# Two layers of attention in one kernel: another order of the steps within a unit of the second layer

## The chip, the cores and the metric

The kernel runs on one core of one Trainium2 chip. The metric is the device time of one execution in microseconds (us). All arithmetic is in 32-bit floats. The engines have short names throughout, as in the profile: PE is TensorE (PEld its loads of weights), DVE is VectorE, ACT is ScalarE, POOL is GpSimd, SP is SyncE, which here only issues transfers.

## The reference

Eight images of 32 x 32 points with 512 channels pass through two layers.

```python
# layer 0: group norm, self-attention with 8 heads of 64 over the 1024 points, projection, residual
x = x + softmax(q k^T / 8) v @ w_out + b_out
# layer 1: deformable attention
x_ln = layernorm(x);  q = x_ln @ wq + bq
o = gelu(depthwise_conv_7x7_stride_2(q) + dw_b)        # 16 x 16 points
offsets = tanh(o @ pw)                                 # two numbers for each of the 256 points
interp = bilinear(x, refs + offsets)                   # 256 sampled points, 4 rows of x for each
k, v = (interp @ wv + bv) @ mk + .., @ mv + ..
z = softmax(qh kh^T) vh @ mo + mo_b + x                # 1024 queries, 256 keys, 8 heads
out = gelu(layernorm(z) @ mlp_w + mlp_b) + z
```

The second layer needs, for each image, the convolution of that image's queries, the offsets, the sampled rows, and from these the keys and values, before its first scores can be made.

## The kernel before, in words

The kernel makes the first layer for all images, writes its result (`mid`) and the normed result (`hat_d`) to memory, and then makes the second layer from these. The change touches the second layer alone (from line 838). The convolution of the first six images is made beside the first layer; that of the last two (`EARLY` is 6) is made in the second, beside the attention.

**Order.** Nothing is scheduled by a planner. Each engine runs its instructions in the order in which the program issues them (`InOrder`, lines 43 to 64; all operations are therefore recorded as line 54). The program makes this order by hand: `at(place, step)` (line 362) puts a step at a place, a number, and `run_due` (line 365) issues the steps by rising place. Equal places go by the order of entry. A step issues everything that it consists of at once, on whichever engines and queues. An engine that waits for something holds up everything behind it on that engine.

**Units.** The second layer has 64 units, numbered n. A unit is one pair of heads (`hp`, 4 of them) of one half image (`hi`, 16 halves of 512 queries). Its steps (`unit_steps`, line 1177) lie at places counted from n:

- n: `scores` (line 97). 32 matmuls into two tiles `sc`, one for each head; on DVE the negated maxima `nmax`, two reductions; on ACT the exponentials `e`, four for each head, with their sums.
- n + 0.02 and n + 0.04: `moved` (line 134) for head 0 and head 1. DVE transposes `e` into `sq` in blocks of 32; SP stores it to memory (`sq_d`) and loads it back, spread over partitions otherwise (`et`). `sq`, `e` and `et` have two buffers, one for each head.
- n + 0.039 and n + 0.041: `share` and `spread` (lines 164, 175): the reciprocal of the sums (`rs`, `rsT`) and its way through memory to `inv`.
- n + 0.06: `query_step` (line 1088): 16 matmuls that make the queries of unit n + 1, and ACT's `q` with its bias.
- n + 1.1 and n + 1.2: `product` (line 150), the matmuls `av` of exponentials and values, and `scale`, DVE's `attH`. These lie in the next unit.

**The end of a tile of rows** (`back_steps`, line 1096). Each unit also takes one tile t of 128 rows of the half image before through the end of the layer. Its places are counted from the tile's own n:

- n + 0.05: `joined` (line 1111): the output projection, 16 matmuls; DVE adds the residual (`z`), takes statistics and the variance (`stats`, `mv`), and POOL raises it to the power -0.5.
- n + 0.13: `norm`: DVE makes `zn`.
- n + 0.6: `turned` (line 1127): four transposes on PE, two copies `zT` on ACT.
- n + 1.03: `mlp`, 16 matmuls; n + 1.035: `biased`, DVE's `res`.
- for two tiles together, `gelu` at 1.72 and `end` at 2.24 after the second tile's n: ACT's gelu (with a table load before and after it), POOL's addition of `z` and the store of the result through POOL's queue.
- `fetch` and `add`, 1.6 and 0.5 ahead of a pair of tiles: SP loads two tiles of `mid` (`xr`) and POOL adds the bias row to them.

The results of matmuls take turns in three buffers `mm`.

**The convolution** (`conv_steps`, line 1204) runs in two lanes of taps, one tap for each of 49 weights. Lane 0 is on DVE, five taps at n + 0.25, or three in units where `points` holds. Lane 1 has seven taps in a unit: four at n + 0.045, three at n + 0.65 and on; each is a product on ACT (`parts`, two buffers) and an addition on POOL (`chunk`).

**The sampled points** (`point_steps`, line 1229). For image b let L = 8b - 4. At L - 0.035 comes the gelu of the convolution `o` on ACT; at L + 0.535 `offsets` (line 970): four pairs of matmuls, the tanh `th` on ACT and two small transposes on PE; at L + 0.75 `targets`, some 22 small operations on DVE (`corners`, line 1019) that make the rows' indices `ii` and weights `wt`. Then for each half h of the points `gather` (line 987), four indirect transfers through POOL's queue into `row` (four buffers), and `sample` (line 997), four DVE operations that add the weighted rows into `smp`: places L + 0.8 and L + 1.22 for the first half, L + 1.23 and L + 2.22 for the second. The keys and values of image b are made from `smp` from L + 3.18 on (`key_step`, `value_step`).

So for image 3, whose stretch is looked at below, L is unit 20.

Of the kernel before, what the change touches and what calls it, by code (L numbers as in the profile page):

```python
# [241 lines left out]
def attention_then_deformable_attention(  # L242
# [48 lines left out]
    def mm_tile():  # L291
        return ps_mm.tile([P, QB], F32, tag="mm", name="mm")
# [69 lines left out]
    def at(place, step):  # L362
        due.append((place, len(due), step))
# [474 lines left out]
    with ExitStack() as l1:  # L838
# [131 lines left out]
        def offsets(b):  # L970
            o = room[b, "o"]
            ps = mm_tile()
            for cb in range(NC):
                nc.tensor.matmul(
                    ps[0:2, 0:NS], lhsT=pww[:, cb, :], rhs=o[:, cb, :],
                    start=(cb == 0), stop=(cb == NC - 1),
                )
            th = cv.tile([2, NS], F32, tag="th", name="th")
            nc.scalar.activation(th, ps[0:2, 0:NS], AF.Tanh)
            room["th"] = mm_tile()[:, 0:4]  # L980
            for h in range(2):
                nc.tensor.transpose(room["th"][:, ts(h, 2)], th[:, ts(h, P)], ident[0:2, 0:2])

        def targets(b):
            room[b, "ii"], room[b, "wt"] = corners(room["th"])
# [24 lines left out]
        def points(b):  # L1010
            conv_load(b)
            conv_gelu(b)
            offsets(b)
            targets(b)
            for h in range(2):
                gather(b, h)
                sample(b, h)
# [78 lines left out]
        def back_steps(hi, start, step, tail=False):  # L1096

            b, half = divmod(hi, 2)
            xs = mid[b].rearrange("(t p e) c -> e t p c", e=2, p=P)[half]
            outs = out_tok[b].rearrange("(t p e) c -> e t p c", e=2, p=P)[half]  # L1100
            xr, z, zn, zT, res = {}, {}, {}, {}, {}
            n_units = 2 * B * NHP

            def fetch(t):
                xr[t] = tmp("xr", 4)
                nc.sync.dma_start(xr[t], xs[t])

            def add(t):
                nc.gpsimd.tensor_tensor(xr[t], xr[t], bo_row, ALU.add)

            def joined(t):
                ps = project(lambda c: attH[hi][:, c, ts(t, P)], lambda c: wo[:, c, :])
                z[t] = tmp("z", 4)
                nc.vector.tensor_tensor(z[t], ps, xr[t], ALU.add)
                stats = work.tile([P, 6], F32, tag="stats", name="stats")
                mv = xr["mv", t] = work.tile([P, 3], F32, tag="mv", name="mv")
                nc.vector.bn_stats(stats, z[t])
                nc.vector.bn_aggr(mv[:, 0:2], stats)
                rstd(mv[:, 2:3], mv[:, 1:2], 1e-5)

            def norm(t):
                zn[t], mv = tmp("zn", 2), xr["mv", t]
                nc.vector.tensor_scalar(
                    zn[t], z[t], mv[:, 0:1], mv[:, 2:3], ALU.subtract, ALU.mult
                )

            def turned(t):
                ps = mm_tile()
                for c in range(NC):
                    nc.tensor.transpose(ps[:, ts(c, P)], zn[t][:, ts(c, P)], ident)  # L1130
                zT[t] = tmp("zT", 2)
                for half in range(2):
                    nc.scalar.copy(zT[t][:, ts(half, C // 2)], ps[:, ts(half, C // 2)])

            def mlp(t):
                res["ps", t] = project(lambda c: zT[t][:, ts(c, P)], lambda c: wm[:, c, :])

            def biased(t):
                res[t] = tmp("res", 3)
                nc.vector.tensor_tensor(res[t], res["ps", t], bm_row, ALU.add)  # L1140

            def gelu(t):
                nc.scalar.activation(res[t], res[t], AF.Gelu)

            def end(t):
                (nc.vector if tail else nc.gpsimd).tensor_tensor(res[t], res[t], z[t], ALU.add)
                (nc.sync if tail else nc.gpsimd).dma_start(outs[t], res[t])

            for t in range(NC):
                over, eve = (start + step * t >= n_units - i and not tail for i in range(2))  # L1150
                n, pair = start + step * t, start + step * (t - t % 2)

                ends = (n + 0.6, n + 1.03, n + 1.035)
                if eve:
                    ends = (n + 0.61, n + 0.72, n + 0.73) if over else (n + 1.06, n + 1.62, n + 1.625)
                places = (pair - 1.6, pair - 0.5), (n + 0.05, n + 0.13), ends
                if tail:
                    turn = n + 0.15 + 0.005 * (t > 0)
                    places = (n - 0.7, n - 0.6), (n, n + 0.01), (turn, n + 0.25, n + 0.26)
                steps = (fetch, add), (joined, norm), (turned, mlp, biased)  # L1160
                for place, what in zip(sum(places, ()), sum(steps, ())):
                    at(place, lambda t=t, what=what: what(t))


                ends = [t - 1, t] if t % 2 and not tail else [t] if tail else []

                for what, after in (
                    (gelu, 0.27 if tail else 0.735 if over else 1.72),
                    (end, 0.28 if tail else 0.74 if over else 2.24),
                ):  # L1170
                    for i in ends:
                        at(n + after, lambda i=i, what=what: what(i))
# [4 lines left out]
        def unit_steps(n):  # L1177
            hi, hp = divmod(n, NHP)
            b = hi // 2
            u = dict(tiles=NQT, at=0, v=lambda j, h: vals[b][:, j, ds((2 * hp + h) * HD, HD)])  # L1180

            def scores():
                u["q"], u["k"] = queries.pop((hi, hp)), keys[b][:, hp, :]
                u["e"] = att.scores(u)

            def scale():
                if hp == 0:
                    attH[hi] = work.tile([P, NHP, QB], F32, tag="attH", name="attH")
                att.scale(attH[hi][:, hp, :], u["inv"])

            at(n, scores)
            at(n + 0.02, lambda: att.moved(u, 0))
            at(n + 0.039, lambda: att.share(u["sums"]))
            at(n + 0.04, lambda: att.moved(u, 1))
            at(n + 0.041, lambda: u.update(inv=att.spread()))
            last = n + 1 == 2 * B * NHP
            at(n + (1.3 if last else 1.1), lambda: att.product(u))
            at(n + (1.305 if last else 1.2), scale)
            if not last:
                at(n + 0.06, lambda: query_step(*divmod(n + 1, NHP)))  # L1200

        def conv_steps():
            for lane, chunks in enumerate(((0, 3, 6), (1, 2, 4, 5, 7))):
                free = 0.5 + lane
                for k in chunks:
                    b, cb = EARLY + k // NC, k % NC
                    first = next(n for n in range(60) if n + 0.49 > free)
                    fills = [first + 0.49, first + 0.55]  # L1210
                    at(fills[0] - 1.8, lambda b=b, cb=cb: conv_fetch(b, cb))
                    for par, place in enumerate(fills):
                        at(place, lambda b=b, cb=cb, par=par: fill(b, cb, par))
                        at(place + 0.02, lambda lane=lane, par=par: fill_end(lane, par))
                    unit = int(fills[1]) + 1
                    i = 0
                    while i < KS * KS:
                        points = unit % (2 * NHP) in range(NHP, NHP + 3)
                        count = 7 if lane else 3 if points else 5
                        for j in range(count):  # L1220
                            if i == KS * KS:
                                break
                            place = 0.25 + 0.01 * j if not lane else 0.045 + 0.001 * j if j < 4 else 0.65 + 0.01 * j
                            at(unit + place, lambda b=b, cb=cb, i=i, lane=lane: tap(b, cb, i, lane))
                            free = unit + place
                            i += 1
                        unit += 1

        def point_steps(b):
# [1 line left out]
            at(last - 1.5, lambda: conv_load(b))  # L1231
            at(last - 0.035, lambda: conv_gelu(b))
            at(last + 0.535, lambda: offsets(b))
            at(last + 0.75, lambda: targets(b))
            for h, (p0, p1) in enumerate(((0.8, 1.22), (1.23, 2.22))):
                at(last + p0, lambda h=h: gather(b, h))
                at(last + p1, lambda h=h: sample(b, h))
            first = 2 * NHP * b
# [79 lines left out]
```

## Time and profile before

| what | us |
|---|---|
| runs: median of 3 (lowest to highest) | 3460.95 (3454.47 to 3464.29) |
| the profiled execution | 3461.8 |
| its span (first to last instruction) | 3459.8 |
| PE busy 0 to 2000 | 1961.68 of 2000 |
| PE busy 2400 to 2600 | 194.36 of 200 |
| PE busy 2600 to 2800 | 181.57 of 200 |
| PE busy 2800 to 3000 | 181.88 of 200 |
| PE busy 3000 to 3400 | 392.69 of 400 |

The second layer's units run from 2233.07 (first scores) to the end. The lanes of taps end early in the stretch from 3000 to 3400.

How to read the profile: the page has one execution. A row of the timeline has the start in us from the beginning of the span, the duration in us, the engine, the line, the operation, the tiles (written <- read), the shape, and the number of instructions that are merged into the row. A bracket at the end gives the idle time before it and what ended that. A row of the waits has who waited for whom, the sum in us, how often, and the longest. The granted clock is the share of full speed that PE was given.

### The profile page before, as it was taken

To read this page: it belongs to the slowest core of one execution; us is meant where nothing else is said; L and a number is where in the kernel's file an instruction comes from. 1 tells how busy PE (TensorE), PEld (TensorE's weight loads), DVE (VectorE), ACT (ScalarE), POOL (GpSimd) and SP (SyncE) were. 2 spreads that over 40 slices of the span, in tenths; PEclk is the share of its full clock that TensorE was granted. 3 is DMA by queue.
4 is the path that set the end of the run, shared out by engine and by line. 5 is a ranking of instruction groups with operands and counts; after the bars stand their busy time and mean duration, and the time that the engine had idled before them with its cause. 6 is when DMAs were issued, how large, how long until landed. Compare 5 with 4: busy or idle time off the path is not lost.

```text
span 3459.8 us, 59748 instructions
## 1 busy us (share of the span) xinstructions
PE 3316.1 (96%) x21736; PEld 1352.4 (39%) x21736; DVE 2540.1 (73%) x3373; ACT 1809.4 (52%) x3919; POOL 1541.1 (45%) x1903
## 2 busy tenths in 40 slices
PE   7999999999999999999999998889998989899998
PEld 3444444444444444344344333333333333333332
DVE  4776787888888888888888884167777667565654
ACT  2443365575576576576576551245555555554442
POOL 1002226646646746746746754034535354532222
PEclk9999999999999999999999999899999999999999
DMA  4666767766766766766766775365656555565653
GB/s 145 174 178 166 208 174 201 210 176 189 216 176 182 226 175 179 229 181 179 217 181 179 214 201 167 126 195 183 209 167 190 164 185 190 177 205 187 218 181 125
DMA packets 446645, 642.57 MB, mean 186 GB/s; under 512 B 77104, under 2 KB 240944, under 8 KB 444304
## 3 DMA queue, kind: packets, MB, share of 16 engines
q1 hardware_dynamic: 415712, 536.67, 53.3%
q0 software_dynamic: 29488, 100.00, 9.5%
q8 instruction: 172, 2.82, 0.3%
q10 hardware_dynamic: 1152, 2.10, 0.2%
q14 instruction: 121, 0.99, 0.1%
HBM read 246.38 MB, written 123.73 MB: 107 GB/s over the span
## 4 chain that ended last, share of the span: by engine, by line
PE 78%; DVE 6%; ACT 5%; DMA 3%; POOL 3%; issue 2%; SPq 2%; DVEq 0%; POOLq 0%; ACTq 0%
PE mm L54 49%; PE sc L54 15%; PE av L54 14%; ACT e L54 3%; SPq L54 2%; POOL chunk L54 1%; DVE nmax L54 1%; DVE sq L54 1%; DMA et<-sq 1%; DVE chunk L54 1%; DMA sq_d<-sq 1%; POOL row L54 1%; DMA et<-sq_d 1%; ACT L54 1%; DMA row<-mid,ii 1%
## 5 line engine op out<-in xcount | busy, mean ns | idle before, releaser
L54 ACT ACTIVATE e<-sc,nmax 128x1024 f32<-128x1024 f32 (+1 forms) x1024 | 803.5, 798 | 574.3 <-DVE nmax L54 573.5
L54 DVE TENSOR_REDUCE nmax<-sc 128x1 f32<-128x1024 f32 (+1 forms) x640 | 751.5, 1215 | 308.5 <-PE sc L54 307.6
L54 DVE STREAM_TRANSPOSE sq<-e 128x1024 f32<-128x1024 f32 x640 | 764.2, 1225 | 246.7 <-ACT e L54 225.4
L54 POOL TENSOR_TENSOR oa<-part_x,oa 128x256 f32<-128x256 f32 x852 | 639.5, 751 | 549.7 <-ACT part_x L54 503.4
L54 ACT ACTIVATE part_x<-pad_x,dww_x 128x256 f32<-128x256 f32 x852 | 441.0, 544 | 251.9 <-POOL oa L54 250.6
L54 PE MATMUL sc<-k,q 64*64 64x512 f32 x4096 | 521.8, 602 | 20.5 <-ACT e L54 10.3
L54 PE MATMUL av<-et,v 128*64 128x256 f32 x4096 | 499.9, 386 | 12.7 <-DMA et<-sq 10.5
L54 PE MATMUL mm<-xT,wqkv 128*64 128x512 f32 x2048 | 463.8, 595 | 3.1 <-issue 3.1
L54 PEld LDWEIGHTS av<-et,v 128*64 128x64 f32 x4096 | 274.7, 137 | 329.1 <-issue 172.7
L54 POOL TENSOR_TENSOR chunk<-parts,chunk 128x256 f32<-128x256 f32 x240 | 180.8, 753 | 384.6 <-ACT parts L54 369.4
L54 POOL TENSOR_TENSOR mv<-mv,minus_half 128x1 f32<-128x1 f32 x128 | 76.0, 594 | 449.8 <-DVE mv L54 449.5
L54 PEld LDWEIGHTS sc<-k,q 64*64 64x64 f32 x4096 | 139.7, 132 | 329.3 <-issue 193.2
L54 PEld LDWEIGHTS mm<-xT,wqkv 128*64 128x64 f32 x2048 | 149.0, 138 | 255.0 <-issue 237.2
L54 PE MATMUL mm<-wm,zT 128*64 128x512 f32 x1024 | 236.0, 603 | 1.0 <-ACT zT L54 1.0
L54 DVE SCALAR_TENSOR_TENSOR od<-pad_x,dww_x,od 128x256 f32<-128x256 f32 x276 | 232.6, 843 | 5.5
L54 PE MATMUL mm<-wqkv,xT 128*64 128x256 f32 x2048 | 232.1, 379 | 0.0
L54 PE MATMUL mm<-wo,attH 128*64 128x512 f32 x1024 | 231.7, 593 | 0.4
L54 PE MATMUL mm<-hat_h,wqq 128*64 128x512 f32 x1024 | 231.5, 594 | 0.0
L54 PE MATMUL mm<-w,attT 128*64 128x512 f32 x1024 | 229.8, 592 | 1.6 <-DVE attT L54 1.6
L54 ACT ACTIVATION_READ_ACCUMULATOR e<-sc,nmax 128x1 f32 x1024 | 209.2, 204 | 0.0
L54 PEld LDWEIGHTS mm<-wqkv,xT 128*64 128x64 f32 x2048 | 147.7, 137 | 78.1 <-issue 6.4
L54 ACT ACTIVATE parts<-pad,dww 128x256 f32<-128x256 f32 x240 | 124.9, 557 | 91.2 <-POOL chunk L54 91.0
(163 smaller groups left out, 3446.8 us busy)
## 6 DMA issues: line engine op xcount, KB each, us to landing
et<-sq SPq DMA_DIRECT2D x2048, 128.0 KB
sq_d<-sq SPq DMA_DIRECT2D x128, 512.0 KB
et<-sq_d SPq DMA_DIRECT2D x128, 512.0 KB
inv<-rs_d SPq DMA_DIRECT2D x256, 128.0 KB
hat_h<-hat_d SPq DMA_DIRECT2D x16, 1024.0 KB
xr<-mid SPq DMA_DIRECT2D x64, 256.0 KB
x<-in_x_dram POOLq DMA_DIRECT2D x60, 256.0 KB
out_dram<-res POOLq DMA_DIRECT2D x60, 256.0 KB
```

Of the source, the lines that this page charges most:

```text
L54: return self.tc.keep_in_program_order(op(*args, **kwargs))
```

## The change

The order of the steps within a unit is changed, and the sampled points come later. From place to place:

- `joined` goes from n + 0.05 to n + 0.012 and `norm` from n + 0.13 to n + 0.03. On PE the projection now stands ahead of `mlp` (n + 0.03); on DVE `z`, its statistics and variance stand ahead of the first `sq`, and `zn` right behind it; POOL's power stands ahead of the four taps.
- `query_step` goes from n + 0.06 to n + 0.042: on ACT the bias of `q` stands ahead of the four taps at n + 0.045.
- `biased` goes from 0.035 to 0.0392: `res` stands behind the reciprocal, ahead of the second `sq`. It still follows its matmuls, which now come second.
- `offsets` is split. The two small transposes are a step of their own, `offsets_turned`, at L + 0.64, behind the turn of the normed tile, and ACT copies their result from PSUM to a tile in SBUF.
- `targets` goes from L + 0.75 to L + 1.041, behind the second `sq`. The gathers go to L + 1.05 and L + 2.05, which is behind the four taps of these units and ahead of the three at 0.65; the samplings go to L + 2.045 and L + 3.045, behind the second `sq` and ahead of `scale`.
- the units with three taps instead of five in lane 0 are one later.

```diff
@@ offsets
-            th = cv.tile([2, NS], F32, tag="th", name="th")
-            nc.scalar.activation(th, ps[0:2, 0:NS], AF.Tanh)
-            room["th"] = mm_tile()[:, 0:4]
+            room["tanh"] = cv.tile([2, NS], F32, tag="th", name="th")
+            nc.scalar.activation(room["tanh"], ps[0:2, 0:NS], AF.Tanh)
+
+        def offsets_turned(b):
+            th = room["tanh"]
+            ps = mm_tile()[:, 0:4]
             for h in range(2):
-                nc.tensor.transpose(room["th"][:, ts(h, 2)], th[:, ts(h, P)], ident[0:2, 0:2])
+                nc.tensor.transpose(ps[:, ts(h, 2)], th[:, ts(h, P)], ident[0:2, 0:2])
+            room["th"] = cv.tile([P, 4], F32, tag="th4", name="th4")
+            nc.scalar.copy(room["th"], ps)
@@ points
             offsets(b)
+            offsets_turned(b)
             targets(b)
@@ back_steps
-                ends = (n + 0.6, n + 1.03, n + 1.035)
+                ends = (n + 0.6, n + 1.03, n + 1.0392)
...
-                places = (pair - 1.6, pair - 0.5), (n + 0.05, n + 0.13), ends
+                places = (pair - 1.6, pair - 0.5), (n + 0.012, n + 0.03), ends
@@ unit_steps
-                at(n + 0.06, lambda: query_step(*divmod(n + 1, NHP)))
+                at(n + 0.042, lambda: query_step(*divmod(n + 1, NHP)))
@@ conv_steps
-                        points = unit % (2 * NHP) in range(NHP, NHP + 3)
+                        points = unit % (2 * NHP) in range(NHP + 1, NHP + 4)
@@ point_steps
-            at(last + 0.75, lambda: targets(b))
-            for h, (p0, p1) in enumerate(((0.8, 1.22), (1.23, 2.22))):
+            at(last + 0.64, lambda: offsets_turned(b))
+            at(last + 1.041, lambda: targets(b))
+            for h, (p0, p1) in enumerate(((1.05, 2.045), (2.05, 3.045))):
```

## The prediction

> **What bounds the kernel now.** I read the page's table of engines first, then TensorE's waits after 2100 us, then the timelines of four units.
>
> ```profile
> PE 3316.1 (96%) x21736; PEld 1352.4 (39%) x21736; DVE 2540.1 (73%) x3373; ACT 1809.4 (52%) x3919; POOL 1541.1 (45%) x1903
> ```
>
> TensorE is busy 96% of the span, so time is won only where it stands still or runs slowly. Its waits in the second pass (total us, times, longest):
>
> ```profile
> PE mm L54 <- DVE zn L54: 47.9, 15, 5.9
> PE av L54 <- DMA et<-sq_d: 13.4, 7, 4.7
> ...
> PE mm L54 <- ACT th L54: 3.7, 8, 0.5
> ...
> PE mm L54 <- DVE smp L54: 1.8, 1, 1.8
> ```
>
> Most of it is the turning of a normed tile (`zn`). TensorE's timeline shows where: units 21 and 22 of the loop (21 is the one after the offsets of image 3, L = 20).
>
> ```profile
> 2626.95 1.89 PE L54 MATMUL av<-et,vals 128*64 128x512 f32 x8
> 2633.64 0.72 PE L54 MATMUL mm<-ident,zn 128*128 128x128 f32 x4 [4.80 <-DVE zn L54]
> 2634.30 3.49 PE L54 MATMUL sc<-keys,q 64*64 64x256 f32 x32
> ...
> 2655.14 1.09 PE L54 MATMUL mm<-ident,zn 128*128 128x128 f32 x4 [5.19 <-DVE zn L54]
> 2656.16 3.69 PE L54 MATMUL sc<-keys,q 64*64 64x256 f32 x32
> ...
> 2672.61 3.80 PE L54 MATMUL mm<-smp,wvk 128*64 128x256 f32 x32
> ```
>
> The 32 score matmuls take 1.96 us in an unhindered unit (2595.90) and 3.49 and 3.69 here: the granted clock is 0.50 from 2655 to 2660. The last line, the keys, came without a wait. Behind all this stand ACT and POOL, which share the taps of the convolution:
>
> ```profile
> 2639.41 0.95 POOL L54 DMA_INDIRECT row<-mid,ii  x1 [0.30 <-DVE nmax L54]
> 2640.38 2.36 POOL L54 TENSOR_TENSOR chunk<-parts,chunk 128x256 f32<-128x256 f32 x3
> ```
>
> ```profile
> 2641.16 0.56 ACT L54 ACTIVATE parts<-pad,dww 128x256 f32<-128x256 f32 x1 [5.26 <-POOL chunk L54]
> 2641.73 1.28 ACT L54 ACT_TABLE_LOAD   x1
> 2643.03 1.15 ACT L54 ACTIVATE res<-res 128x512 f32<-128x512 f32 x2
> 2644.18 1.28 ACT L54 ACT_TABLE_LOAD   x1
> ```
>
> The third product of a group of three (`parts` has two buffers) waits for POOL's first add, that add stands behind the gathers in POOL's queue, and the exponentials stand behind the third product on ACT. So POOL's queue sets when the exponentials begin.
>
> **The change, part by part.** S is the start of a unit's scores. An unhindered unit has its product with the values at S+12.23 and its turn due at S+14.05 (2581.26, 2593.49, 2595.31), and lasts 14.64.
>
> Removed. *zn* comes after the first `sq` instead of after both. The projection now ends at S+5.3, `z`, its statistics and POOL's power take 2.5 (2590.35 to 2592.82), and `zn` is there soon after S+8.6, or after the exponentials of head 0 and one `sq`. Of the 15 waits, those with ordinary units behind them go. In unit L the tanh lies beside the turn (0.58), so the 7 waits of 0.46 go: 3.2. The slow matmuls after the waits: from turn to projection an undisturbed unit takes about 5.94 (2595.31, 2595.90, 2597.79, 2601.27); in the fifteen places the excess adds up to 20.0 (1.62 after 4.80; 2.94, 2.60, 2.60 and 2.87 after 5.19, 5.90, 5.59 and 3.96). All that could go: 47.9 + 3.2 + 20.0 = 71.1.
>
> Unit L+1. ACT now does the query's bias before the taps, so in unit L the four products start at S+13.2, POOL's adds end at 13.9 + 3.15 = 17.05; the two `res` adds, two stores and two `xr` adds take 6.8 (2612.11 to 2618.90); one add 0.8, third product 0.55: the exponentials of L+1 start at 25.2 of unit L, which lasts 16.7, so at S+8.5 (before: S+10.6, behind the indices on DVE). Head 0 takes 1.8, `sq` 1.25, `zn` 0.55: S+12.1, before the turn. **No wait.**
>
> Unit L+2. Both heads end at S+12.1 of L+1; reciprocal, its transpose, bias, second `sq`: 2.3; the index arithmetic, now behind them, 3.9 (2619.83 to 2623.78): S+18.3, which is S+3.7 of L+2. Four gathers, 5.2 (2624.06 to 2629.26), now stand *ahead* of the group of three adds: 8.9; add 0.8 and third product 0.55: 10.3; two table loads and two gelus, 3.75: exponentials at S+14.0, `zn` at 14.0 + 1.8 + 1.25 + 0.55 = 17.6. **3.6 us of wait remain** (5.2 to 5.9 before), three times, and some 2.0 once for image 2 with fewer adds: 12.8. L+3 starts at 18.2.
>
> Unit L+3. The exponentials of L+2 end at 17.6; bias and first product 1.2, four adds 3.15: 21.95; the second four gathers 5.2; `res`, stores, `xr` 6.8; one add and third product 1.35: 35.3, that is S+17.1 of L+3 (before S+9.0, since the gathers lay elsewhere). Exponentials 3.6, the 2.3 to the second `sq`: 23.0. Only then DVE samples the second half: four operations, 2.85 alone (2634.01 to 2636.85), and I add 0.6 for POOL's adds beside it (five taps 3.26 instead of 2.56): 26.4. The keys are due at S+14.05: **a new wait of 12.4 us**, in images 2 to 5: 49.6. Queued behind the keys on TensorE are the values, the turn and the next scores; nothing passes. Image 1 has no gelu and no stores: its exponentials start at S+10.3 in L+2, and 3.6 + 1.2 + 3.15 + 5.2 + 2.5 + 1.35 later, at S+12.7, in L+3; sampled at 22.05: a wait of 8. Images 6 and 7 have no taps on ACT; there `xr` lies behind gathers and stores until S+7.9, so `z` to second `sq` ends at 13.7, sampling at 16.5: 2.5 each, 5. Sum 62.6. Bounds of one wait of 12.4: 0 if the exponentials start right after the maxima (S+4.4); 15.7 with sampling at its slow 5.85 (2655.52 to 2661.37), gathers at 5.6, `res` to `xr` at 7.3.
>
> Slow matmuls after the new waits: 1.6 after each of four short ones, 2.75 (mean of the four rows above) after five long ones, 0.6 after two: 21.4.
>
> The Trainium skill, "TensorE: Matmul & The Clock Gate", section on what's actually happening, says that the clock halves after an idle window of about 3.4 us and returns after 3.4 busy ones. By that an estimate is 1.7 per wait over 3.4 and none below, so about 14 instead of 21.4, though 1.61 was lost at 2456.49 after a wait of 1.22. The skill's "SBUF — State Buffer", section on who interferes with whom, says that a VectorE operation with two inputs in SBUF is fully blocked by a GpSimd one that reads there; if four adds blocked sampling wholly, each long wait would be 2.5 longer, 10 in all. The taps' rows show a milder effect.
>
> Covered or small. The units with three instead of five taps on DVE move from L..L+2 to L+1..L+3: 1.0 us more ahead of the maxima of L+1, which then end near S+4.5, in the shadow of the exponentials' wait until S+8.5; without that cover it would cost up to 1.0 per image. The copy of the turned offsets is new on ACT; nearest rows are the tanh, 0.37, and a product, 0.53; it lies in POOL's wait: between 0 and +0.4 in each of 8 images, taken as 0. Moving four DVE operations ahead of `sq` delays the first half's store by up to 2.1 (S+6.5 to 8.6). SyncE's queue has the first `et` behind the store, and it waits for the product at S+14.2 anyway; the second store is queued behind that, so most units pay nothing. But in units 43 to 55 the first `et` comes at S+16 to 21, behind its store, and `av` waited 0.65 and 1.31 there. Ends: -3 (nothing added, those two gone) and +20 (2.1 in nine such units, and the last product, whose 4.5 of wait grow too). I take +5: 3 and 2.
>
> **Sum.** New 12.8 + 62.6 + 21.4 + 5.0 = 101.8; old 71.1; +30.7. The profiled execution took 3461.8 (span 3459.8): 3492.5. The median of the runs, 3460.95, is 0.9 lower, less than I can resolve.
>
> **Rivals.**
> *Faster: the exponentials aren't held.* For it: POOL is busy only 45%, and the keys had no wait before. Against it: the 5.26 above, at the same place in the queues. If the L+3 exponentials start by S+5, the keys find their data, and the 71.1 go, but for up to 19 that L+2 keeps (12.8 and four times 1.6): 3391 to 3410. If they start by S+9.5 the waits fall to about 4.8 and all is even; that is the point from which this rival decides.
> *About even*: the four long waits at 2.1 to 7.3 each, 3451 to 3472.
> *Worse*: slow sampling and gathers with store waits at their upper end: 4 x 3.3 + 15 more: 3521.
> That the order isn't what is said can be excluded: in the built program the gathers stand ahead of the adds and the sampling ahead of the scaling, in every image.
>
> **How the numbers follow.** Forecast case (3472 to 3510): 0.64; worse (to 3530): 0.11; even: 0.07; faster: 0.18. The likeliest time is 3492.5. The range from 3450 to 3522 leaves out the fast rival and the end of the worse one, with 0.2 between them. A measurement of this kernel can tell about 0.3% from no change, 10 us; faster 0.18, same 0.07, slower 0.75.
>
> **What would show it.** Right: TensorE's waits for `zn` fall from 47.9 to about 13 and the tanh line goes; "mm <- DVE smp" rises from 1.8 to 50 to 70 in eight or fewer waits; third products wait 15 us for POOL in L+2 to L+3; sampling ends near S+26. Wrong: keys that start at S+14 in L+3, or exponentials there before S+9.5; or waits for `et` in most units, which would show that the later `sq` does cost.

## The result and the profile after

The changed kernel takes 3483.12 us (median of six runs, 3477.66 to 3491.43), the kernel before 3462.18 (six runs beside them, 3454.47 to 3466.8): a ratio of 1.0064, interval 1.0048 to 1.008. It is slower, by about 21 us where 30.7 were forecast. The profiled execution took 3483.09, its span is 3481.4, against 3459.8 before: 21.6 more.

From the page of the changed kernel, the table of engines (busy us, share of the span, instructions):

```profile
PE 3319.0 (95%) x21736; PEld 1357.6 (39%) x21736; DVE 2473.5 (71%) x3373; ACT 1808.9 (52%) x3927; POOL 1542.9 (44%) x1903
```

TensorE's matmuls are the same number and busy 2.9 us longer. The other 18.7 are time in which it stands still, and its waits after 2100 us say for whom (total us, times, longest):

```profile
PE mm L54 <- DVE smp L54: 45.2, 7, 10.7
PE av L54 <- DMA et<-sq_d: 22.1, 9, 4.7
PE mm L54 <- DVE zn L54: 15.5, 4, 4.9
...
PE mm L54 <- ACT th L54: 0.9, 2, 0.5
```

The waits for `zn` fell from 47.9 to 15.5, and those for the tanh from 3.7 to 0.9. In their place stand the keys' waits for the sampled points: 45.2, of which 42.7 lie in the loop (10.62, 9.31, 10.71 and 10.13 in images 2 to 5, 1.14 and 0.81 in images 7 and 1) and the rest in the preparation. The waits for `et` rose by 8.7, and those of the scores for the queries `q` fell by 2.2 (3.5 to 1.3).

Image 3 shows how one unit after another is affected. L is unit 20, and its units have these lengths, from scores to scores:

| unit of image 3 | L | L+1 | L+2 | L+3 | sum |
|---|---|---|---|---|---|
| before | 18.47 | 19.93 | 21.86 | 24.20 | 84.46 |
| after | 16.67 | 14.64 | 19.52 | 36.50 | 87.33 |
| exponentials begin, before | S+8.2 | S+10.6 | S+11.2 | S+9.0 | |
| exponentials begin, after | S+9.0 | S+8.8 | S+14.7 | S+17.2 | |

L and L+1 gain 7.1 us, L+2 gains 2.3, and L+3 gives back 12.3. TensorE's timeline of L+2 and L+3 after the change (start, us, what; the bracket is the idle time before the row and what ended it):

```profile
2657.14 1.09 PE L54 MATMUL mm<-ident,zn 128*128 128x128 f32 x4 [4.38 <-DVE zn L54]
2658.15 3.69 PE L54 MATMUL sc<-keys,q 64*64 64x256 f32 x32
...
2672.48 2.44 PE L54 MATMUL av<-et,vals 128*64 128x512 f32 x7
...
2675.18 0.61 PE L54 MATMUL mm<-smp,wvk 128*64 128x256 f32 x2
2685.11 5.59 PE L54 MATMUL mm<-smp,wvk 128*64 128x256 f32 x28 [9.31 <-DVE smp L54]
```

The keys of image 3, which had found their data before the change, stand still for 9.31 us and then run slowly (5.59 us for 28 matmuls, where the 32 of before took 3.80; the granted clock is 0.52 from 2685 to 2690). What held the points is read backwards. First POOL's timeline of the same stretch:

```profile
2658.26 3.54 POOL L54 TENSOR_TENSOR chunk<-parts,chunk 128x256 f32<-128x256 f32 x4 [7.13 <-ACT parts L54]
2661.95 1.27 POOL L54 DMA_INDIRECT row<-mid,ii  x1 [0.15 <-issue]
...
2671.67 2.50 POOL L54 TENSOR_TENSOR xr<-xr,bo_row 128x512 f32<-128x512 f32 x2
2674.12 2.35 POOL L54 TENSOR_TENSOR chunk<-parts,chunk 128x256 f32<-128x256 f32 x3
```

Between the four adds and the three stand the gathers (2661.95 to 2667.27), then `res`, two stores and `xr` (to 2674.12): 12.2 us of other work in POOL's queue. ScalarE waits for just that:

```profile
2674.89 0.53 ACT L54 ACTIVATE parts<-pad,dww 128x256 f32<-128x256 f32 x1 [12.48 <-POOL chunk L54]
2675.32 0.45 ACT L54 ACTIVATE e<-sc,nmax 128x256 f32<-128x256 f32 x1
```

The third product waits 12.48 us for POOL's first add to free a `parts` buffer, and the exponentials begin right behind it, at S+17.2. VectorE makes the two `sq` from them, and only then samples the second half:

```profile
2681.18 0.82 DVE L54 TENSOR_SCALAR smp<-row,wt 128x512 f32<-128x512 f32 x1
2682.04 3.01 DVE L54 SCALAR_TENSOR_TENSOR smp<-row,wt,smp 128x512 f32<-128x512 f32 x3
```

It ends at 2685.05, S+26.9, and the keys start. So the gathers, now ahead of the group of three adds, hold the exponentials, and the sampling, now behind the second `sq`, takes over their lateness. The same gathers hold the sampling by a second path too, which is only 2.5 us shorter: `xr` stands behind them in POOL's queue, `z` waits 5.55 us for it on VectorE (to 2672.98), and `z` with its statistics (to 2674.80) stands ahead of both `sq`. The exponentials let the first `sq` start at 2677.27.

### The profile page after: what moved, and what is told of

The parts are those of the page before. It is cut to its first block, busy times and chain, and to the rows that moved or that the text cites. A ratio compares the mean times of both kernels' runs of the same rounds, so it can differ in the third digit from the quotient of the medians.

```text
span 3481.4 us, 59722 instructions
## 1 busy us (share of the span) xinstructions
PE 3319.0 (95%) x21736; PEld 1357.6 (39%) x21736; DVE 2473.5 (71%) x3373; ACT 1808.9 (52%) x3927; POOL 1542.9 (44%) x1903
## 4 chain that ended last, share of the span: by engine, by line
PE 74%; ACT 7%; DVE 5%; POOL 4%; DMA 4%; issue 3%; SPq 2%; another core or an unknown queue 0%; DVEq 0%; POOLq 0%; ACTq 0%
PE mm L54 47%; PE sc L54 14%; PE av L54 13%; ACT e L54 4%; SPq L54 2%; DVE sq L54 2%; DMA et<-sq 1%; DVE nmax L54 1%; DMA sq_d<-sq 1%; POOL chunk L54 1%; DVE smp L54 1%; DMA et<-sq_d 1%; POOL xr L54 1%; ACT L54 1%; POOL res L54 1%
## 5 line engine op out<-in xcount | busy, mean ns | idle before, releaser
L54 PE MATMUL av<-et,v 128*64 128x256 f32 x4096 | 499.8, 386 | 17.4 <-DMA et<-sq 13.3
```

What stands on the lines that cost most here:

```text
L54: return self.tc.keep_in_program_order(op(*args, **kwargs))
```

## The experiments

All edits are given against the changed kernel. The ratios are to the kernel before, run beside each.

| kernel | median us (range) | ratio (interval) |
|---|---|---|
| changed | 3483.12 (3477.66 to 3491.43) | 1.0064 (1.0048 to 1.008) |
| order_alone | 3431.81 (3427.86 to 3433.31) | 0.9913 (0.989 to 0.9936) |
| points_alone | 3520.05 (3512.41 to 3522.55) | 1.0169 (1.0141 to 1.0196) |
| gather_behind_taps | 3454.89 (3448.39 to 3461.2) | 0.9987 (0.9975 to 1.0) |
| sample_first | 3430.5 (3424.85 to 3433.29) | 0.991 (0.9885 to 0.9934) |
| offsets_alone | 3468.22 (3458.98 to 3475.62) | 1.0014 (1.0 to 1.0028) |
| fewer_taps | 3440.11 (3435.7 to 3442.99) | 0.9936 (0.9917 to 0.9955) |
| order_fewer_taps | 3420.87 (3419.53 to 3428.04) | 0.9888 (0.9869 to 0.9907) |
| sample_fewer_taps | 3424.84 (3418.7 to 3429.7) | 0.9897 (0.9879 to 0.9915) |
| norm_alone | 3437.33 (3427.0 to 3439.64) | 0.9915 (0.9888 to 0.9942) |
| sample_between | 3420.38 (3420.1 to 3420.6) | 0.9874 (0.9853 to 0.9895) |

The theory is the one of the prediction: the queues of POOL and VectorE carry the loss, the new order of projection and norm is a gain. The main rival was that the later transposes of exponentials (and with them the store and `et`) cost the time.

**order_alone**: the new order of projection, norm, query and bias stays, the points go back to their places.

```diff
-                        points = unit % (2 * NHP) in range(NHP + 1, NHP + 4)
+                        points = unit % (2 * NHP) in range(NHP, NHP + 3)
...
-            at(last + 1.041, lambda: targets(b))
-            for h, (p0, p1) in enumerate(((1.05, 2.045), (2.05, 3.045))):
+            at(last + 0.75, lambda: targets(b))
+            for h, (p0, p1) in enumerate(((0.8, 1.22), (1.23, 2.22))):
```

> The changed kernel with the index arithmetic, gathers, samplings and the three-tap units at their old places (0.75; 0.8 and 1.22, 1.23 and 2.22); the order of projection, norm, queries and bias, and the split offsets, stay. The queue theory (the loss is the keys waiting for samples that stand behind exponentials that stand behind gathers in POOL's queue): keys don't wait, zn waits fall from 47.9 to 15 to 25 in units L+1 and L+2, 3425 to 3445. The rival that the later transposes of exponentials cost (their stores and loads come later): waits of the products for et rise and the time is 3462 or more.

It is faster than the kernel before by 0.9%, within the range expected. Its two largest waits of TensorE in the second layer:

```profile
PE av L54 <- DMA et<-sq_d: 22.3, 13, 4.6
PE mm L54 <- DVE rs L54: 10.7, 3, 3.6
```

The second line is the wait of the turn, put down to the instruction behind `zn` on VectorE: three waits, and one of 2.3 for `zn`, where the kernel before has fifteen of 47.9 together. Five waits of 6.6 us together for `res` are new. The waits for `et` are as long as in the changed kernel. So the later transposes cost some 9 us of waiting (22.3 against 13.4) and the slow matmuls behind it, and still this half of the change is a gain of 29 us: as the cause of the loss, the rival falls.

**points_alone**: the other half, with projection, norm, query and bias back at their places.

```diff
-                ends = (n + 0.6, n + 1.03, n + 1.0392)
+                ends = (n + 0.6, n + 1.03, n + 1.035)
...
-                places = (pair - 1.6, pair - 0.5), (n + 0.012, n + 0.03), ends
+                places = (pair - 1.6, pair - 0.5), (n + 0.05, n + 0.13), ends
...
-                at(n + 0.042, lambda: query_step(*divmod(n + 1, NHP)))
+                at(n + 0.06, lambda: query_step(*divmod(n + 1, NHP)))
```

> The changed kernel with projection, norm, queries and bias at their old places; the later points and the split offsets stay. The queue theory: the exponentials of L+2 and L+3 are as late as in the changed kernel, and zn, now again behind both transposes, waits for them too, so it is slower than the changed kernel: 3495 to 3525, with zn waits of 70 to 100. The rival that the order does the harm: 3455 to 3470.

It is 1.7% slower than before. The points' new places cost 59 us by themselves, and here the cost shows as waits for `zn`:

```profile
PE mm L54 <- DVE zn L54: 98.7, 18, 10.3
```

The keys wait for nothing in its loop: in image 3 TensorE has stood still 10.32 and 5.76 us at the turns before them. Against the same runs of before (3460.63) order_alone is 29 us below and points_alone 59 above, 30 together, where the whole is 21 above. The split of `offsets` is in both halves and so counted twice (by offsets_alone, below, it is 0 to 10 us slower by itself), so whether the halves also hide each other's time can't be told.

**gather_behind_taps**: the gathers go behind the three adds of their units.

```diff
-            for h, (p0, p1) in enumerate(((1.05, 2.045), (2.05, 3.045))):
+            for h, (p0, p1) in enumerate(((1.715, 2.045), (2.715, 3.045))):
```

> The changed kernel with both gathers issued behind the group of three taps of their unit (places 1.715 and 2.715 instead of 1.05 and 2.05), the samplings unmoved. The queue theory: exponentials of L+2 start some 5 us earlier (near S+8) and of L+3 too, zn waits go to 0 to 5, the keys' waits fall from about 10 to 6 to 9, 3445 to 3462. The rival that only the sampling's place behind the second transpose matters and POOL's queue does not: 3475 to 3490, keys' waits as before.

It is 28 us below the changed kernel: the whole loss goes, and the waits for `zn` with it. The time is as expected, but the keys' waits hardly fall:

```profile
PE mm L54 <- DVE smp L54: 44.4, 6, 10.5
```

In the loop they are 5.71, 8.99, 8.93, 10.48 and 8.06 in images 1 to 5: 9.1 in the mean of images 2 to 5, where the changed kernel has 10.2 and 6 to 9 were expected, and image 1 has 5.71 instead of 0.81. In image 3 the exponentials of L+3 start at S+12.7 instead of S+17.2, and the second half is sampled at S+24.3 instead of S+26.9; but L+3 itself begins without the wait and the slow matmuls of L+2, so its keys are due sooner. POOL's queue shows where the gathers stand now:

```profile
2659.43 2.41 POOL L54 TENSOR_TENSOR chunk<-parts,chunk 128x256 f32<-128x256 f32 x3
2662.00 1.02 POOL L54 DMA_INDIRECT row<-mid,ii  x1 [0.15 <-issue]
...
2666.81 0.58 POOL L54 TENSOR_TENSOR mv<-mv,minus_half 128x1 f32<-128x1 f32 x1
```

Of the 12 us that lay ahead of the three adds the gathers were 5; `res`, the stores and `xr` (2652.11 to 2659.43) stay there. And the gathers now hold something else: POOL's power `mv` stands behind them and ends at 2667.39, `zn` starts at 2667.43, and the second `sq` and the sampling follow `zn` on VectorE.

**sample_first**: the samplings go ahead of what they stood behind, and the second gathers follow the first sampling.

```diff
-            for h, (p0, p1) in enumerate(((1.05, 2.045), (2.05, 3.045))):
+            for h, (p0, p1) in enumerate(((1.05, 2.015), (2.016, 2.3))):
```

> The changed kernel with the first half sampled ahead of both transposes of L+2 (2.015), the second half gathered at once behind it (2.016) and sampled at 2.3, in the same unit's end. Queue theory and the rival of the sampling's place: the keys find their samples, no wait at the keys, zn waits of 12 to 25 stay (the first gather still stands ahead of the three taps), 3425 to 3445. The rival of the later transposes: 3470 or more.

As expected. The keys have no wait for their samples in the loop, L+3 of image 3 lasts 23.41 instead of 36.50, and a wait of 5.63 for the turn stands in L+2 (23.0 in all images, 12 to 25 expected): 53 us less than the changed kernel, by the places of two steps on VectorE's and POOL's queues.

**offsets_alone**: of the whole change only the split of `offsets` is kept; these are the edits of order_alone and points_alone together.

```diff
-                ends = (n + 0.6, n + 1.03, n + 1.0392)
+                ends = (n + 0.6, n + 1.03, n + 1.035)
...
-                places = (pair - 1.6, pair - 0.5), (n + 0.012, n + 0.03), ends
+                places = (pair - 1.6, pair - 0.5), (n + 0.05, n + 0.13), ends
...
-                at(n + 0.042, lambda: query_step(*divmod(n + 1, NHP)))
+                at(n + 0.06, lambda: query_step(*divmod(n + 1, NHP)))
...
-                        points = unit % (2 * NHP) in range(NHP + 1, NHP + 4)
+                        points = unit % (2 * NHP) in range(NHP, NHP + 3)
...
-            at(last + 1.041, lambda: targets(b))
-            for h, (p0, p1) in enumerate(((1.05, 2.045), (2.05, 3.045))):
+            at(last + 0.75, lambda: targets(b))
+            for h, (p0, p1) in enumerate(((0.8, 1.22), (1.23, 2.22))):
```

> The kernel before with the split offsets alone (transposes behind the turn of the normed tile, the copy to SBUF on ACT). Every theory: the seven waits of 0.46 for the tanh go in the loop and nothing else changes, 3455 to 3463. If the copy in the preparation costs, the first scores start later than 2233.07 by up to 1.5.

A miss: no gain, 1.0014 (1.0 to 1.0028), and a median 5 us above the expected range. Six of the seven waits of 0.46 for the tanh are gone (image 1 keeps its own, as no tile is turned in its unit L), but the waits for `zn` rise from 47.9 to 54.0. TensorE's timeline in unit L of image 3 has this:

```profile
2616.11 0.63 PE L54 MATMUL mm<-ident,zn 128*128 128x128 f32 x4 [1.94 <-DVE zn L54]
```

The turn starts 1.94 us after the products of the offsets end (2614.17). In the kernel before it was 1.96 (2611.84 to 2613.80), with the 0.46 for the tanh inside. `zn` sets the turn in both, so what a wait ahead of it gives is lost at the next. The 3.2 us that the prediction put down as removable by the split were not there to be won, as long as `zn` is late. The first scores start at 2235.86, 2.8 later than before; but in the other kernels with this same preparation they start anywhere between 2233.35 and 2241.13, so a price of the copy in the preparation can't be read from it.

**fewer_taps**: lane 1 has five taps instead of seven in units L+1 and L+2, so that POOL's second group there is one add; the other taps come in later units.

```diff
-                        count = 7 if lane else 3 if points else 5
+                        two = unit % (2 * NHP) in range(NHP + 1, NHP + 3)
+                        count = (5 if two else 7) if lane else 3 if points else 5
```

> The changed kernel with five taps in lane 1 instead of seven in units L+1 and L+2: the second group has one tap, not three, so no product in it waits for an addition behind the gathers. The taps left out come in later units; the sum of work is the same, and the gathers and samplings stay where the change put them. The queue theory: the exponentials of L+2 start near S+9 instead of S+14.7 and those of L+3 at S+8 to 12 instead of S+17.2, zn waits go to 0 to 3, the four long keys' waits fall to 4 to 8, 3440 to 3460. The rival that the sampling's place and not the products' wait holds the exponentials: exponentials as late as before, 3478 to 3486.

With one product in the second group none waits for POOL behind the gathers. The exponentials of image 3 start at S+8.5, S+7.5 and S+6.7 in L+1 to L+3 (S+8.8, 14.7 and 17.2 in the changed kernel), and the time falls by 43 us. That is the strongest evidence for the queue: every gather and sampling is where it was and the work is the same; only two products a unit, one of which waited for the queue, are elsewhere. The waits of TensorE after 2100 us:

```profile
PE av L54 <- DMA et<-sq_d: 36.4, 14, 5.3
PE mm L54 <- DVE smp L54: 14.1, 6, 6.2
```

In the loop the keys' waits are down to 7.9 from 42.7 (one of 6.2 lies in the preparation), and the turn has none. But the exponentials of L+3 come 10.5 us earlier and the sampling ends only 4.5 us earlier, at S+22.4. VectorE's timeline of L+3 in image 3 shows the second path from POOL's queue:

```profile
2656.12 0.69 DVE L54 TENSOR_TENSOR z<-mm,xr 128x512 f32<-128x512 f32 x1 [6.28 <-POOL xr L54]
```

`z` waits for `xr`, which stands behind the gathers, until S+14.1, and both `sq` and the sampling stand behind `z`. The waits for `et` rise to 36.4 from 22.1. In L+3 of image 3 TensorE waits 3.47 us for it, where it was not late at all. It belongs to the second `sq` of L+2, whose store stands behind these two in SyncE's queue:

```profile
2638.98 0.32 SPq L54 DMA_DIRECT2D sq_d<-sq  x1
2645.31 0.37 SPq L54 DMA_DIRECT2D et<-sq_d  x1
```

The load is issued 6.3 us after the store on which it waits; in the changed kernel it was 2.65 (2656.59 to 2659.24). In images 2 to 5 it is 6.3 to 8.0 against 2.65 to 3.4. With earlier exponentials the store follows the loads of `xr` by 1.5 to 3.7 us, where it followed by 7.8 to 10.4; whether it shares their time, or that of the gathers, was not tried.

**order_fewer_taps**: order_alone, and five taps in units L and L+1, where its gathers are.

```diff
-                        points = unit % (2 * NHP) in range(NHP + 1, NHP + 4)
-                        count = 7 if lane else 3 if points else 5
+                        points = unit % (2 * NHP) in range(NHP, NHP + 3)
+                        two = unit % (2 * NHP) in range(NHP + 0, NHP + 2)
+                        count = (5 if two else 7) if lane else 3 if points else 5
...
-            at(last + 1.041, lambda: targets(b))
-            for h, (p0, p1) in enumerate(((1.05, 2.045), (2.05, 3.045))):
+            at(last + 0.75, lambda: targets(b))
+            for h, (p0, p1) in enumerate(((0.8, 1.22), (1.23, 2.22))):
```

> The new order with the old places of the points (as in order_alone), and five taps instead of seven in lane 1 in units L and L+1. The queue theory: what order_alone had left, exponentials at S+12 to 14 in L+1 to L+3 and their waits for rs and zn (about 3.6 each), goes for the most part, 3412 to 3425. If these waits come from the index arithmetic on DVE alone, it stays at 3428 to 3434.

The time is as expected, and 1.1% faster than the kernel before. The waits did not go for the most part: those of the turn are 7.4 in three (2.4 to 2.5 each), down from 10.7 (3.6 each) and the one of 2.3; image 3 takes 74.99 us (16.67, 17.11, 17.41, 23.80) against 84.46.

**sample_fewer_taps**: sample_first with the taps of fewer_taps.

```diff
-                        count = 7 if lane else 3 if points else 5
+                        two = unit % (2 * NHP) in range(NHP + 1, NHP + 3)
+                        count = (5 if two else 7) if lane else 3 if points else 5
...
-            for h, (p0, p1) in enumerate(((1.05, 2.045), (2.05, 3.045))):
+            for h, (p0, p1) in enumerate(((1.05, 2.015), (2.016, 2.3))):
```

> The changed kernel with the samplings ahead (as in sample_first) and five taps instead of seven in lane 1 in units L+1 and L+2. The queue theory: exponentials of L+2 and L+3 start at S+8 to 11 instead of S+11 to 15, the waits at the turn of 4.4 to 6.1 go, 3410 to 3425. The rival as above: 3426 to 3434.

The time lies at the upper end of what was expected, and the mechanism expected was wrong: the exponentials of L+2 are early (S+7.5), but the turn of that unit still waits 5.42. VectorE's timeline of L+2 in image 3:

```profile
2634.82 0.75 DVE L54 SCALAR_TENSOR_TENSOR smp<-row,wt,smp 128x512 f32<-128x512 f32 x1 [0.67 <-DMA row<-mid,ii]
2635.49 1.24 DVE L54 STREAM_TRANSPOSE sq<-e 128x1024 f32<-128x1024 f32 x1
```

Each operation of the sampling but the first waits for its rows, the last until 2634.82, and `sq` and `zn` (2636.65) stand behind it, with their data long there. The wait was the rows', not the exponentials'.

**norm_alone**: order_alone, with the query's bias and `res` also back at their old places; only `joined` and `norm` stay moved, and the split.

```diff
-                ends = (n + 0.6, n + 1.03, n + 1.0392)
+                ends = (n + 0.6, n + 1.03, n + 1.035)
...
-                at(n + 0.042, lambda: query_step(*divmod(n + 1, NHP)))
+                at(n + 0.06, lambda: query_step(*divmod(n + 1, NHP)))
```

(and the places of the points as in order_alone)

> As order_alone, but with the queries and the bias at their old places too: only projection and norm go ahead of the transposes (and the offsets are split). If these two carry the order's gain, it is as fast as order_alone, 3427 to 3438. If the queries' place has a share in it, slower, 3440 or more.

As expected: 0.9915, where order_alone has 0.9913. The projection and the norm carry the whole gain, as far as these runs can tell. The scores have ten waits for the queries, 17.0 in all, where order_alone has two of 1.3 together, but `et` waits 15.8 instead of 22.3; a difference between the two can't be told.

**sample_between**: the sampling of the first half behind `zn` and ahead of the reciprocal, the second gather right after it, and the taps of fewer_taps.

```diff
-                        count = 7 if lane else 3 if points else 5
+                        two = unit % (2 * NHP) in range(NHP + 1, NHP + 3)
+                        count = (5 if two else 7) if lane else 3 if points else 5
...
-            for h, (p0, p1) in enumerate(((1.05, 2.045), (2.05, 3.045))):
+            for h, (p0, p1) in enumerate(((1.05, 2.035), (2.036, 2.3))):
```

> As sample_fewer_taps, with the first sampling behind zn and ahead of the second transpose (2.035, second gather 2.036) instead of ahead of zn (2.015). The queue theory: the turn's waits of about 5.5 in L+2 (16 to 21 in all, put down to rs) go, since zn no longer stands behind the sampling; the keys stay without long waits: 3400 to 3415. If those waits came from late exponentials instead, it stays at 3419 to 3430.

It is the fastest of all with 3420.38, level with order_fewer_taps, and some 5 us above the expected range. The time alone would fit the rival (3419 to 3430), but the turn's waits, which the rival would have kept, are gone, and L, L+1 and L+2 of image 3 take 16.67, 14.64 and 14.64. What stayed is in L+3 (28.34), on VectorE:

```profile
2643.52 1.49 DVE L54 TENSOR_SCALAR smp<-row,wt 128x512 f32<-128x512 f32 x1
2645.04 6.56 DVE L54 SCALAR_TENSOR_TENSOR smp<-row,wt,smp 128x512 f32<-128x512 f32 x3
```

The second half's sampling takes 8.05 us here, alone 2.85, and the maxima of L+3 (2651.53) stand behind it, so the exponentials start at S+16.9. And the first half's sampling, which waits for rows, now stands ahead of `res`: TensorE has seven waits of 13.3 us together for `res` to empty a buffer `mm`, which the changed kernel has not. Four of them, 8.4 us, come early in L+3, behind that sampling: there the wait for the rows has moved from `zn` to `res`. The other three, 1.6 each, lie among the keys, behind the late exponentials.

## Why the prediction was right, and where its sizes were off

**Side and mechanism** were right. The exponentials of image 3 were put at S+8.5, S+14.0 and S+17.1 in L+1 to L+3; they start at S+8.8, 14.7 and 17.2. The sampling was to end at S+26.4 and ends at S+26.9. L+1 has no wait. L+2 keeps 4.38 (3.6 forecast). Of the signs that were named, the line "mm <- DVE smp" rose to 45.2, short of 50 to 70, and the third products of image 3 wait 7.59 in L+2 and 12.48 in L+3, where 15 was named. gather_behind_taps and fewer_taps show that the gathers in POOL's queue and the product that waits behind them make the exponentials late and, with that, the turn of L+2; with either of the two moved away the loss is gone. The keys' wait needs the late sampling as well: it stays near 9 in gather_behind_taps, and goes in sample_first.

| term, us | forecast | measured |
|---|---|---|
| `zn` that remains | 12.8 | 15.5 |
| keys | 62.6 | 42.7 |
| later `sq`: `et`, end | 5.0 | 8.7 |
| slow matmuls | 21.4 | 23.9, as what is left over |
| new in all | 101.8 | 92.7 (21.6 + 71.1) |

(The waits for the tanh fell by 2.8 instead of 3.2, and the first scores of the second layer come 1.5 later; both are taken off the remainder. It still holds the 2.2 by which the waits for the queries fell, and was not told apart further.)

**The keys' term failed in size**, by 20 us. Three steps of it:

- In images 2 to 5 the wait is 10.2 in the mean, not 12.4. "The keys are due at S+14.05" held for a unit that runs at full speed, but L+3 begins behind a wait for `zn`. Its scores took 3.69 (1.96 unhindered), its projection 4.01 (3.65), and the product with the values came at S+14.33 (2672.48 less 2658.15) instead of S+12.23. These 2.1 us were counted twice, as slow matmuls and again inside the wait that swallows them.
- The key matmuls were treated as one block. The first four of 32 come before the wait, in two rows of 0.6 each, one of which is shown above.
- Image 1 was put at 8 and has 0.81. The exponentials of its L+3 are where they were expected (S+12.9, forecast 12.7), but ahead of the keys TensorE waits 4.13 for `et`. Images 6 and 7 were put at 2.5 each and have 0 and 1.14; in image 6 a wait of 2.38 for `et` stands ahead of the keys.

**The later `sq`** was too low, 5 for 8.7, and partly in other places than named: units 43 to 55 got 2.3 (forecast 3) and the end lost 0.6 (forecast +2), but unit 4 got 2.8 and unit 7, in image 1, 4.13. **The split of `offsets`** was credited with 3.2; offsets_alone shows that alone it gives nothing. In the changed kernel, where `zn` of unit L is early, six of the seven waits are gone (2.8). **The copy on ScalarE** was taken as 0; it lasts 0.18.

**The chances**: the faster rival was to win if the L+3 exponentials started before S+5, and even was S+9.5. Both bounds left out the second path: in fewer_taps the exponentials start at S+6.7, but `z` waits for `xr` until S+14.1 and the sampling ends at S+22.4; the time is 3440. In sample_first the keys find their samples, and 3430.5 is still above the 3391 to 3410 given for that case; its longest waits are those for `et` (19.4) and at the turn (16.3 and 4.4).

**The clock.** The forecast charged 1.6 after each of four short waits; it had rows of before for that (1.62 lost after 4.80, 1.61 after 1.22). That is no price for a short wait: six other waits for `zn` in the kernel before, of 1.22 to 1.69 us, are followed by scores of 1.96, at full speed (in image 3 at a granted clock of 1.00 from 2614 to 2618). After the change a wait of 1.90 in image 2 is followed by scores of 3.48 instead of 1.96, at a granted clock of 0.59 from 2498 to 2502: 1.5 lost. The Trainium skill, "TensorE: Matmul & The Clock Gate", section "What's actually happening", puts the drop behind an idle window of about 3.4 us; read as a threshold for one wait, the slow matmuls would have been an estimated 14. The 1.5 lost after 1.90 speaks against that reading, and the remainder of 23.9 lies nearer to the forecast's 21.4. What decides after a short wait stays open.

## What to carry to other kernels

When a step is moved in hand-ordered queues, follow each instruction that it issues to what then stands behind it on its engine: here four gathers ahead of three adds held a product in a two-buffer tile, that product held the exponentials on ScalarE, and the exponentials held the sampling, three engines away. Follow every path: `xr` behind the same gathers held `z`, and `z` the same sampling, so where the exponentials came 10.5 us earlier, the sampling came only 4.5. A step that waits for a transfer belongs behind everything on its engine whose data is there already, or what follows inherits the wait (`zn`, then `res`); but not behind work that is itself late, as the changed kernel's sampling was. And a slow stretch that ends in front of a longer wait is not an added cost: count either the one or the other.

## What the runs showed of the hardware that was not expected

**Sampling beside POOL's additions.** The four operations take 2.85 alone. Beside the adds of taps (128x256), as in the changed kernel, 3.87: three of them have two tensors and take 3.01 together instead of 2.33. In sample_between POOL's timeline beside them is this:

```profile
2643.28 1.45 POOL L54 TENSOR_TENSOR res<-res,z 128x512 f32<-128x512 f32 x1
...
2645.66 1.29 POOL L54 TENSOR_TENSOR res<-res,z 128x512 f32<-128x512 f32 x1
...
2647.85 2.51 POOL L54 TENSOR_TENSOR xr<-xr,bo_row 128x512 f32<-128x512 f32 x2
2650.31 0.73 POOL L54 TENSOR_TENSOR chunk<-parts,chunk 128x256 f32<-128x256 f32 x1
```

From 2643.52 to 2651.04 POOL adds for 5.7 us (1.21, 1.29, 2.51 and 0.73), and the sampling takes 5.2 longer than alone. The three operations with two tensors take 6.56 instead of 2.33, 4.2 longer beside 4.5 us of additions. That is nearly full exclusion. The Trainium skill, "SBUF — State Buffer", section "Who interferes with whom", states that a VectorE operation with two inputs in SBUF contends with a GpSimd one that reads there, and calls the shared ports an exclusive lock. Beside the tap adds the four operations lost only about 1.0 in 2.5 us of overlap, far from exclusion; why the two differ was not tried.

**Hidden transfers.** With the exponentials early, the way of `sq` through memory to `et` comes to the surface: 13.4 us of waits before, 36.4 in fewer_taps, 18.5 in the fastest kernel, where it is the longest line of TensorE's waits. The way itself is also slower where the store comes close behind the loads of `xr` (6.3 to 8.0 us from store to load in fewer_taps, 2.65 to 3.4 in the changed kernel, L+2 of images 2 to 5).
